# TensorE's opening filler: products of a cleared tile in place of transposes of the identity

## The chip, the cores and the metric

The kernel runs on one core of one Trainium2 chip. The metric is the device time of one execution in microseconds (us), as the median of several runs; the profile is a further execution, recorded by the hardware profiler, with a time of its own. Engines are named as in the profile: PE is TensorE's matmul, PEld its weight load, DVE is VectorE, ACT ScalarE, POOL GpSimd and SP the engine that issues most transfers.

## The reference

A stack of four graph layers over `x` of 128 batches, 128 nodes and 512 features, with one 128x128 matrix `adj`, all in float32. After each layer comes a layer norm of the sum:

```python
x = _layernorm(x + _L0_gnn_ref(x, adj, weight, bias))      # (adj @ x) @ W + bias
x = _layernorm(x + _L1_gnn_ref(x, W, a, beta, adj))        # graph attention, one head, masked by adj, elu
x = _layernorm(x + _L2_gnn_ref(x, adj, adj, b))            # max over nodes of relu(adj @ x + b)
x = _layernorm(x + _L3_gnn_ref(x, w_qkv, w_proj, ...))     # 8-head attention, masked by adj, projection, norm
```

For the opening of the kernel only the first layer counts: `y = einsum('nm,bmd->bnd', adj, x)`, then `einsum('bnd,do->bno', y, weight)`.

## The kernel before, in words

A batch is one tile of 128 partitions (nodes) by 512 features. Every batch is a chain of steps, written as a Python generator (`batch`) that yields a request for an engine with an estimated duration. A planner, `Plan.run`, serves the requests at build time in the order of its estimates, and so fixes the order of instructions on PE, DVE, ACT, POOL and SP. Each engine works through its own list in that order and waits on semaphores only for data and for free buffers. There are eight PSUM banks (`ps`).

The opening of the kernel runs like this. POOL builds a 128x128 identity, `ident`, with `make_identity` (a memset, then an affine select). SP issues the load of `adj` (`loads`, line 340), then those of the first weight `w0` in four chunks, while ACT's queue issues the load of batch 0 of `x` (line 332). `adjacency` (lines 388 to 402) takes a PSUM bank that nothing reads, calls `fill(10)`, and then transposes `adj_sb` on TensorE (line 395); `fill(2)` follows it in PE's list. DVE copies the transpose out of PSUM to `adjT` (line 398).

`mixed` (line 263) makes `adj @ x` of a batch, turned: four products of 128x128 by 128x128 (line 268), copied out of PSUM to `yT`. For batch 0 (`first`) there is again a `fill(2)` behind the products in PE's list, and DVE copies one half of `yT` (line 274) and ACT the other (line 276). `product` (line 260) then multiplies `yT` by `w0`, four products with 512 columns, each behind the landing of its chunk of `w0`.

`fill(n)` (line 383) issues n transposes of `ident` into the idle bank; nobody reads what they write:

```python
        for i in range(n):
            nc.tensor.transpose(idle[0][:, i % K, :], ident, ident)
```

The profile counts hardware instructions: a float32 product of the source is two of them (the four of line 268 for one batch are x8 in the timeline), each with a weight load of its own; a transpose is one (`fill(10)` is x10).

The requests of `adjacency` and `mixed` carry fixed durations (2.0 us for the opening on PE) that do not depend on what `fill` issues.

Of the kernel before, what the change touches and what calls it, by code (L numbers as in the profile page):

```python
# [8 lines left out]
F32 = mybir.dt.float32  # L9
# [6 lines left out]
P = 128  # L16
D = 512
K = D // P
# [30 lines left out]
class Plan:  # L49
# [14 lines left out]
    def use(self, engine, work, take=None, late=0.05, urgent=False, follow=False):  # L64

        names = take if callable(take) else lambda: (take,) if take else ()  # L70
        return engine, work, names, late, 0 if follow else 1 if urgent else 2
# [4 lines left out]
    def done(self, event, late=0.0):  # L76
        event.left -= 1
        event.at = max(event.at, self.now + late)
        if not event.left:
            for r in event.chains:  # L80
                r["ready"] = max(r["ready"], event.at)
                self.step(r, None)

    def give(self, slot):
        name, i = slot
        self.slots[name][i] = self.now
# [52 lines left out]
def gnn_stack_kernel(  # L139
# [17 lines left out]
    nc = tc.nc  # L157
# [3 lines left out]
    const = ctx.enter_context(tc.tile_pool(name="const", bufs=1))  # L161
# [8 lines left out]
    def buf(slot, *shape):  # L170
        return work.tile([P, *shape], F32, name="{}_{}".format(*slot))

    def bank(slot, *shape):

        p = ps.tile([P, D], F32, name="{}_{}".format(*slot))
        if len(shape) == 1:
            return p[:, : shape[0]]
        return p.rearrange("p (a b) -> p a b", a=shape[0])
# [84 lines left out]
    def mixed(xb, nodes, first=False):  # L263

        b0, b1 = yield use("PE", 0.9, lambda: ("ps", "yT"), late=0.2)
        p = bank(b0, K, P)
        for k in range(K):
            nc.tensor.matmul(p[:, k, :], xb[:, k * P : (k + 1) * P], nodes, start=True, stop=True)  # L268
        yT = buf(b1, K, P)
        if first:  # L270
            fill(2)

            yield use("DVE", 0.35, late=0.0)
            nc.vector.tensor_copy(yT[:, : K // 2], p[:, : K // 2])  # L274
            yield use("ACT", 0.05, urgent=True)
            nc.scalar.copy(yT[:, K // 2 :], p[:, K // 2 :])
        else:
            yield use("ACT", 0.6, urgent=True)
            nc.scalar.copy(yT, p)  # L279
        give(b0)  # L280
        return yT, b1
# [7 lines left out]
        nc.sync.dma_start(dst, scratch.rearrange("(a r) c f -> (r c) a f", a=Q))  # L289


    ident = const.tile([P, P], F32, name="ident")
    make_identity(nc, ident)
    neghalf = const.tile([P, 1], F32, name="neghalf")
# [86 lines left out]
    idle = []  # L381

    def fill(n):

        for i in range(n):
            nc.tensor.transpose(idle[0][:, i % K, :], ident, ident)  # L386

    def adjacency():
        b0 = yield use("PE", 2.0, "ps")
        idle.append(bank(b0, K, P))  # L390
        fill(10)
        yield adj_in
        b1 = yield use("PE", 0.3, "ps", late=0.2, urgent=True)
        p = bank(b1, K, P)
        nc.tensor.transpose(p[:, 0, :], adj_sb, ident)  # L395
        fill(2)
        yield use("DVE", 0.3)
        nc.vector.tensor_copy(adjT, p[:, 0, :])
        give(b1)
        done(adj_ready)  # L400
        give(b0)
        yield scalars_in
        yield use("DVE", 1.2)
        nc.vector.tensor_copy(adj_cols, adj_sb.rearrange("p (r c) -> p c r", c=Q))
        nc.vector.tensor_copy(ident_cols, ident.rearrange("p (r c) -> p c r", c=Q))
        nc.vector.tensor_scalar(
            maskb, adj_cols.rearrange("p c r -> p (c r)"), 0.0, MASKED,
            op0=ALU.is_equal, op1=ALU.mult,
        )
        nc.vector.tensor_scalar(  # L410
            beta_id, ident_cols.rearrange("p c r -> p (c r)"), beta1_sb, None, op0=ALU.mult
        )
# [273 lines left out]
    def batch(i):  # L686
# [5 lines left out]

        yield adj_ready
        yT, by = yield from mixed(xb, adjT, i == 0)
        biased = Event()
        plan.start(pool_add(xb, bias0_sb, biased, bias0_in), i)
# [19 lines left out]

        yield gr.attention[h]
        yT, by = yield from mixed(xb, gr.eT[h][:, b % 2])
        gr.read(h, 2)
        bp = yield use("PE", 3.44, "ps", late=0.2)  # L720
# [204 lines left out]
    with tc.manual_schedule(  # L925
        engines={ENG.PE, ENG.DVE, ENG.Activation, ENG.Pool, ENG.SP}
    ):
        plan.start(loads(), 0)
        plan.start(adjacency(), 0)
        for i in range(NB):  # L930

            plan.start(batch(i), early(i))
        plan.run()
# [27 lines left out]
```

## Time and profile before

| | |
|---|---|
| median of 4 runs | 3243.22 us (3243.09 to 3243.61) |
| profiled execution, time | 3243.25 us |
| profiled execution, span (first to last instruction) | 3241.5 us |
| PE busy | 3229.5 us of the span, 12831 instructions |
| PEld busy | 1724.3 us |
| DVE, ACT, POOL busy | 2660.8, 1176.2, 950.7 us |
| mean granted TensorE clock | 0.999 |

The span is 1.75 us shorter than the execution's time; the rest lies before the first and after the last instruction. The profiled execution stands within 0.03 us of the median. In a timeline row the first number is the start in us from the span's start, the second the time from the start of the row's first instruction to the end of its last (they overlap), then engine, line, operation, output<-inputs, shapes and the number of instructions; in brackets is the idle time before it and what ended it.

### The profile page before, as it was taken

Reading aid. Unit: us, or ns where it says so; the run is one execution under the profiler, and the core shown is the slowest. Engines: PE = TensorE matmul, PEld = TensorE weight load, DVE = VectorE, ACT = ScalarE, POOL = GpSimd, SP = SyncE. Lnnn points to the kernel's source line nnn. Section 1 sums busy time; section 2 is a strip of 40 time slices with the busy share of each in tenths; the row PEclk is TensorE's granted clock in tenths of the full one; section 3 lists DMA queues with packets and bytes.
Section 4 is the critical chain, followed back from the end, with each engine's and each line's share of the span. In section 5 each row is a group of like instructions: output and inputs, shape, how many; then the busy total and the mean of one; then the engine's idle time right before and its main releaser. Section 6 shows DMA issues by size and latency. Waiting matters only on the chain.

```text
span 3241.5 us, 40472 instructions
## 1 busy us (share of the span) xinstructions
PE 3229.5 (100%) x12831; PEld 1724.3 (53%) x12831; DVE 2660.8 (82%) x5677; ACT 1176.2 (36%) x3449; POOL 950.7 (29%) x1033
## 2 busy tenths in 40 slices
PE   9999999999999999999999999999999999999998
PEld 5655555545555455554555545555555555556565
DVE  7888788888888888888888888888787887888877
ACT  2433334333333333332333423334233342343332
POOL 3222223232232322323223232232232332233222
PEclk9999999999999999999999999999999999999999
DMA  4233322323323233232332323322333223332332
GB/s 173 55 97 106 106 75 77 101 91 106 92 70 98 94 106 92 70 95 95 106 104 65 88 95 107 101 71 82 99 104 107 71 77 101 99 111 66 116 88 96
DMA packets 469893, 304.27 MB, mean 94 GB/s; under 512 B 319280, under 2 KB 401584, under 8 KB 469680
## 3 DMA queue, kind: packets, MB, share of 16 engines
q1 hardware_dynamic: 469536, 301.42, 31.2%
q8 instruction: 103, 1.69, 0.2%
q14 instruction: 110, 0.90, 0.1%
q10 hardware_dynamic: 144, 0.26, 0.0%
HBM read 158.93 MB, written 142.67 MB: 93 GB/s over the span
## 4 chain that ended last, share of the span: by engine, by line
PE 100%; DVE 0%; POOL 0%; ACT 0%; issue 0%; POOLq 0%; DVEq 0%; ACTq 0%
PE ps L260 54%; PE ps L573 27%; PE ps L268 7%; PE ps L622 4%; PE ps L643 4%; PE ps L738 3%; PE ps L876 0%; PE ps L386 0%; ACT v L818 0%; POOL rstd L203 0%; PE ps L431 0%; DVE x L906 0%; DVE st L910 0%; POOLq L957 0%; PE ps L395 0%
## 5 line engine op out<-in xcount | busy, mean ns | idle before, releaser
L260 PE MATMUL ps<-w_sb,yT 128*128 128x512 f32 x2048 | 902.5, 592 | 0.2 <-DVE yT L274 0.2
L573 PE MATMUL ps<-xT,wqkv_sb 128*128 128x512 f32 (+1 forms) x2304 | 886.4, 545 | 0.0
L203 POOL TENSOR_TENSOR rstd<-ve,neghalf 128x1 f32<-128x1 f32 x640 | 436.0, 682 | 1152.2 <-DVE ve L197 942.3
L573 PEld LDWEIGHTS ps<-xT,wqkv_sb 128*128 128x128 f32 x2304 | 437.7, 190 | 446.8 <-issue 421.4
L260 PEld LDWEIGHTS ps<-w_sb,yT 128*128 128x128 f32 x2048 | 384.2, 190 | 458.6 <-issue 441.6
L260 PE MATMUL ps<-wqkv_sb,xT 128*128 128x512 f32 x1024 | 451.4, 593 | 0.0
L260 PE MATMUL ps<-wproj_sb,v 128*128 128x512 f32 x1016 | 445.5, 595 | 0.7 <-ACT v L818 0.7
L788 ACT ACTIVATE qkT<-qkT,nmx 128x128 f32<-128x128 f32 x1008 | 389.0, 389 | 16.4 <-DVE nmx L774 16.4
L189 DVE BATCH_NORM_STATS2 st<-x 128x6 f32<-128x512 f32 x510 | 347.3, 681 | 18.0 <-ACT x L746 15.1
L582 ACT ACTIVATE qkT<-ps 128x512 f32<-128x512 f32 (+1 forms) x144 | 77.4, 549 | 707.4 <-PE ps L573 707.4
L253 POOL TENSOR_TENSOR x<-x,v 128x512 f32<-128x512 f32 x127 | 174.1, 1371 | 516.4 <-DVE v L837 516.1
L260 PEld LDWEIGHTS ps<-wproj_sb,v 128*128 128x128 f32 x1016 | 190.7, 190 | 233.8 <-issue 229.9
L260 PEld LDWEIGHTS ps<-wqkv_sb,xT 128*128 128x128 f32 x1024 | 191.8, 190 | 227.8 <-issue 223.2
L253 POOL TENSOR_TENSOR x<-x,bias_sb 128x512 f32<-128x512 f32 x128 | 180.9, 1427 | 429.4 <-PE ps L268 419.1
L223 ACT ACTIVATE x<-x,nmr,rstd 128x512 f32<-128x512 f32 x257 | 206.6, 810 | 200.8 <-DVE nmr L221 194.8
L279 ACT COPY yT<-ps 128x512 f32<-128x512 f32 x255 | 147.6, 584 | 275.6 <-PE ps L268 275.6
L798 DVE STREAM_TRANSPOSE pt<-qkT 128x1024 f32<-128x1024 f32 x128 | 158.5, 1238 | 79.5 <-DMA p_d<-pt 79.2
L253 POOL TENSOR_TENSOR x<-x,beta_sb 128x512 f32<-128x512 f32 x128 | 163.0, 1274 | 186.6 <-DVE xt L753 142.6
L710 DVE SCALAR_TENSOR_TENSOR scr<-x,wa_rows 128x512 f32<-128x512 f32 x256 | 185.0, 722 | 26.3 <-ACT x L223 21.5
L788 ACT ACTIVATION_READ_ACCUMULATOR qkT<-qkT,nmx 128x1 f32 x1008 | 190.1, 189 | 0.0
L767 DVE TENSOR_TENSOR qkT<-ps,maskb 128x512 f32<-128x512 f32 x256 | 160.1, 681 | 29.2 <-PE ps L622 29.2
L726 ACT ACTIVATE ex<-ps 128x512 f32<-128x512 f32 x128 | 76.2, 595 | 241.1 <-PE ps L260 238.8
(86 smaller groups left out, 3513.9 us busy)
## 6 DMA issues: line engine op xcount, KB each, us to landing
p_d<-pt SPq DMA_DIRECT2D x128, 512.0 KB, 2.8
qkT<-p_d SPq DMA_DIRECT2D x128, 512.0 KB, 4.3
x_d<-xt SPq DMA_DIRECT2D x128, 256.0 KB, 2.3
xT<-x_d SPq DMA_DIRECT2D x512, 64.0 KB, 2.4
x<-in_x SPq DMA_DIRECT2D x127, 256.0 KB, 2.6
out<-x SPq DMA_DIRECT2D x127, 256.0 KB, 2.0
z<-s_d SPq DMA_DIRECT2D x64, 128.0 KB, 2.9
e_d<-et SPq DMA_DIRECT2D x64, 128.0 KB
```

The source lines that it names most:

```text
L189: nc.vector.bn_stats(st, src)
L203: nc.gpsimd.tensor_tensor(rstd, ve, neghalf, op=ALU.pow)
L223: nc.scalar.activation(xb, xb, AF.Identity, bias=nmr, scale=rstd)
L253: nc.gpsimd.tensor_tensor(dst, dst, other, op=ALU.add)
L260: nc.tensor.matmul(p, lhs(k), rhs(k), start=(k == 0), stop=(k == K - 1))
L268: nc.tensor.matmul(p[:, k, :], xb[:, k * P : (k + 1) * P], nodes, start=True, stop=True)
L279: nc.scalar.copy(yT, p)
L573: nc.tensor.matmul(p[:, j, :], wqkv_sb[:, k, (c + j) * P : (c + j + 1) * P], gr.xT[:, k, : gr.size * P], start=(k == 0), stop=(k == K - 1),)
L710: nc.vector.scalar_tensor_tensor(scr, xb, 1.0, wa_rows[:, j, :], op0=ALU.mult, op1=ALU.mult, accum_out=gr.s[:, b, j : j + 1],)
L767: nc.vector.tensor_tensor(pr[:, j * K : (j + 1) * K], sc[j], maskb[:, None, :].to_broadcast([P, K, P]), op=ALU.add,)
L788: nc.scalar.activation(pr[:, j, :], pr[:, j, :], AF.Exp, bias=nmx[:, j : j + 1], accum_out=sums[:, j : j + 1],)
L798: nc.vector.transpose(pt.rearrange("p c h s -> p h c s"), pr.rearrange("p h (c r) -> p h c r", c=Q))
```

## The change

A tile `zeros` of 128x128 is allocated and cleared by DVE ahead of everything else. `fill` issues products of `zeros` with its own first 64 columns in place of transposes of `ident`. The three calls of it grow from 10, 2 and 2 to 12, 3 and 3. The order of all other instructions, on every engine, is as before; DVE's list has the memset in front.

```diff
+    zeros = const.tile([P, P], F32, name="zeros")
+    nc.vector.memset(zeros, 0.0)
     ident = const.tile([P, P], F32, name="ident")
     make_identity(nc, ident)
...
     def fill(n):
 
         for i in range(n):
-            nc.tensor.transpose(idle[0][:, i % K, :], ident, ident)
+            nc.tensor.matmul(
+                idle[0][:, i % K, : P // 2], zeros, zeros[:, : P // 2], start=True, stop=True
+            )
 
     def adjacency():
         b0 = yield use("PE", 2.0, "ps")
         idle.append(bank(b0, K, P))
-        fill(10)
+        fill(12)
         yield adj_in
         b1 = yield use("PE", 0.3, "ps", late=0.2, urgent=True)
         p = bank(b1, K, P)
         nc.tensor.transpose(p[:, 0, :], adj_sb, ident)
-        fill(2)
+        fill(3)
...
         yT = buf(b1, K, P)
         if first:
-            fill(2)
+            fill(3)
```

## The prediction

> **What bounds the kernel now.** I read the page first: busy time, then the chain that ended last.
>
> ```profile
> span 3241.5 us, 40472 instructions
> PE 3229.5 (100%) x12831; PEld 1724.3 (53%) x12831; DVE 2660.8 (82%) x5677; ACT 1176.2 (36%) x3449; POOL 950.7 (29%) x1033
> PE 100%; DVE 0%; POOL 0%; ACT 0%; issue 0%; POOLq 0%; DVEq 0%; ACTq 0%
> ```
>
> PE is the chain. The table of waits for PE alone says where it ever stood still:
>
> ```profile
> PE ps L386 <- POOL ident masks.py:199: 1.4, 1, 1.4
> PE ps L260 <- ACT v L818: 0.7, 1, 0.7
> PE ps L876 <- ACT v L818: 0.7, 1, 0.7
> PE ps L260 <- DVE yT L274: 0.2, 1, 0.2
> ```
>
> These are 3.0 us in all: two at the start and two in the last twenty microseconds. Between 7.25 and 3222 us PE never waits, so whatever the change does to the moment at which the first product of L260 starts (7.25 us) is handed to the end one for one, and it can do nothing else: the filler stands only ahead of that moment. The question is when that product starts. The timeline of PE and of its weight loads over the opening, with two rows from further down:
>
> ```profile
> 1.39 2.39 PE L386 MATMUL ps<-ident 128*128 128x128 f32 x10 [1.39 <-POOL ident masks.py:199]
> 3.80 0.18 PEld L395 LDWEIGHTS ps<-ident,adj_sb 128*128 128x128 f32 x1 [0.43 <-DMA adj_sb<-in_adj]
> 3.80 0.47 PE L395 MATMUL ps<-ident,adj_sb 128*128 128x128 f32 x1
> 4.07 0.63 PE L386 MATMUL ps<-ident 128*128 128x128 f32 x2
> 4.32 0.29 DVE L398 COPY adjT<-ps 128x128 f32<-128x128 f32 x1 [4.32 <-PE ps L395]
> 4.66 2.08 PE L268 MATMUL ps<-adjT,x 128*128 128x128 f32 x8
> 6.53 0.53 PE L386 MATMUL ps<-ident 128*128 128x128 f32 x2
> 6.78 0.42 DVE L274 COPY yT<-ps 128x256 f32<-128x256 f32 x1 [2.17 <-PE ps L268]
> 7.25 0.30 PEld L260 LDWEIGHTS ps<-w_sb,yT 128*128 128x128 f32 x2 [0.49 <-DVE yT L274]
> 10.79 2.84 PE L268 MATMUL ps<-adjT,x 128*128 128x128 f32 x24
> 3228.91 3.72 PE L876 MATMUL ps<-wproj_sb,v 128*128 128x256 f32 x16 [0.74 <-ACT v L818]
> ```
>
> The reader is to see a slow clock in the opening. The same products of L268 take 2.84 us for 24 at 10.79 us (one takes 0.275, so 23 steps of 0.111) and 2.08 us for 8 at 4.66 us: steps of 0.213 between all but the first two. The transposes step by 0.213 too. The trace's record of the granted clock begins at 6.81 us, with full clock; ahead of that it has no record, so the page's clock row shows full there as well, and the steps are the better witness. I call 0.213 cold and 0.111 warm.
>
> **The filler's start.** It waits for DVE's memset, not for `ident`. After the same opening barrier POOL starts its memset of the same shape at 0.73 us, for 0.20; DVE has nothing ahead of its own. 0.73 + 0.20, and 0.05 from POOL's end to the first transpose as seen, gives 0.98 us, 0.4 earlier than 1.39 (bounds 0.85 to 1.08, by DVE rows of this shape of 0.1 less or more). DVE's first other work is at 4.32, so the memset costs nothing there.
>
> **What one filler costs.** This decides. A product of the source is two instructions, so `fill(12)` is 24 where there were 10, and each `fill(3)` is 6 where there were 2. Each has a weight load and a moving pass, and the load of the next runs beside the pass of this one, so the step is the longer of the two. The pass follows the width: 16 products of 256 columns took 3.72 us (0.216 each, warm), 128 columns 0.111, so 64 columns would be 0.054 warm and 0.107 cold. The load does not shrink: the stationary side is still all 128 columns. The two loads at 7.25 us, which nothing delays, span 0.30 us at 0.19 for one: the second begins 0.11 after the first, so a warm product load holds the path 0.11, and cold twice that, 0.21. So I take 0.111 warm and 0.213 cold for each, as if the width had not been halved. The other bound is the pass, 0.054 and 0.107. I am near the load since every product has one and its row is of the very same size.
>
> [...]
>
> **The opening, added up.** Cold, 24 fillers end at 0.98 + 24 x 0.213 = 6.09 us. In the trace before, `adj` is there at 3.80 us and its transpose starts then; the new filler stands in front of it in PE's list. If the clock rises at time R, then (R - 0.98)/0.213 fillers ran cold and the rest take 0.111 each. From the filler's end F on, all warm: transpose 0.11, six fillers 0.67, so L268 starts at F + 0.78 (the copy to `adjT` would allow 0.65: transpose 0.27, DVE 0.29, 0.09 for two hand-overs; the fillers are late). Then 8 x 0.111 = 0.89, and the half copy of `yT` ends 0.16 + 0.04 + 0.42 later and hands over in 0.05: 1.56; the six fillers behind them end at 0.89 + 0.67 = 1.56, the same. So L260 starts at F + 2.34, against 7.25 before.
>
> When is R? The trace bounds it. Before, the clock rose 5.43 us after the first transpose but only 2.15 us after the first product (4.66). If products alone count, R is 0.98 + 2.15 = 3.13 us; if the moment belongs to the chip's own pacing, or all PE work counts alike, it is 6.4 to 6.8. I take the middle of 3.13 and 6.81, 4.97 us, being near to neither: 18.7 fillers cold, 5.3 warm, F = 5.55, L260 at 7.89: 0.64 us later than before. At R = 3.13: 10.1 cold, 13.9 warm, F = 4.67, L260 at 7.01, 0.24 earlier. At R = 6.81: F = 6.09, the next six fillers begin at 6.36, two run cold and four warm, L268 starts at 7.24 and L260 at 8.80, 1.55 later.
>
> [...]
>
> What else moves: the loads of `w0` and `x` have the same issue order; a later PE finds them landed. The identity leaves the filler's start and becomes a second wait of L395, which it precedes by more than 2 us. The order on every engine is otherwise unchanged. So the sum is 3243.25 + 0.64 = 3243.9 us, and by the median of 3243.22 the same.
>
> A difference under 0.2% (6.5 us) can't be told from no change here; all cases below are inside it.
>
> **The rivals.** *One, the clock does not come earlier* (products of zeros, with the array moving half the time, count no more than transposes did, or the moment isn't the program's to choose): the change then doesn't do what it says, and the 24 fillers at 0.213 hold `adj`'s transpose from 3.80 to 6.09. Price +1.55 us, 3244.8. For it: the loads fill half of each step. Against: PE is busy without a gap from 0.98 on. It decides when R is later than 6.1. *Two, the filler is as cheap as its width* (0.107 cold): 24 end at 3.55, before `adj` is there, and the clock is up by then or soon after. L395 starts at 3.80 as before, L268 0.65 later, L260 at 6.01 at best, 1.24 earlier; batch 2 of `x`, which landed at 10.62 and whose products would be wanted at 10.44, takes 0.2 of that back. Price -1.1, 3242.1. For it: 0.43 us of PE's weight queue stood idle before 3.80, room that such a filler fits. Against: the load's row above. *Three, slower than can be missed*: the new tile shifts the addresses of all tiles behind it; if that cost 2 ns on each of PE's 12831 steps, 26 us, the kernel would be slower by 0.8%. It decides from 0.5 ns a step on (6.5 us). Nothing in the trace points to it; steps of one shape at different buffers agree to 1 or 2 ns.
>
> **How the numbers follow.** My forecast (load price, R between 3.1 and 6.1, -0.25 to +1.2): 0.57. Rival one: 0.25. Rival two: 0.16. Rival three: 0.02. The range leaves out the lower half of rival two and the far end of rival one and adds 0.25 for the scatter of the runs: 3242.4 to 3245.1. Faster by over 0.2%: 0.01; within: 0.97; slower: 0.02.
>
> **What would show it.** In the profile after: the first filler near 0.98 us; two weight loads per filler at steps of 0.21 and then 0.11, no step near 0.05; L395 starting clearly behind 3.80, at 4.7 to 6.1; L268's 8 products in about 1.05 us, not 2.08; L260 at 7.0 to 8.8; the record of the clock beginning ahead of 6.81. L395 still at 3.80 with idle time before it would make the price wrong; L268 still at 2.08 us would make the clock wrong; any difference beyond 7.25 to 3222 us would make the frame wrong.

## The result and the profile after

The changed kernel takes 3246.86 us (median of 41 runs, 3246.03 to 3247.56) against 3243.13 us of the kernel before in 61 runs alternating with it (3242.21 to 3245.01): ratio 1.0011, interval 1.0007 to 1.0016. It is 3.7 us slower, nearly six times the forecast difference, under the 0.2% that the prediction called a change but clear of the scatter (the two sets of runs do not overlap), and above the stated range of 3242.4 to 3245.1. The profiled execution took 3246.89 us with a span of 3245.1 us, 3.64 us more than the one before.

PE's waits show that the frame of the prediction holds. The only one left in the opening is the memset; the two near the end stand as before:

```profile
PE ps L388 <- DVE zeros L293: 1.1, 1, 1.1
PE ps L880 <- ACT v L822: 0.7, 1, 0.7
PE ps L260 <- ACT v L822: 0.7, 1, 0.7
```

The timeline of the opening after (lines moved: the filler is L388, `adj`'s transpose L399, the copy to `adjT` L402):

```profile
0.83 0.17 DVE L293 MEMSET zeros<- 128x128 f32 x1 [0.83 <-PEq L952]
1.05 5.38 PE L388 MATMUL ps<-zeros 128*128 128x64 f32 x24 [1.05 <-DVE zeros L293]
6.23 0.42 PE L399 MATMUL ps<-ident,adj_sb 128*128 128x128 f32 x1
6.44 1.38 PE L388 MATMUL ps<-zeros 128*128 128x64 f32 x6
7.61 2.02 PE L268 MATMUL ps<-adjT,x 128*128 128x128 f32 x8
9.43 1.38 PE L388 MATMUL ps<-zeros 128*128 128x64 f32 x6
10.60 3.97 PE L260 MATMUL ps<-w_sb,yT 128*128 128x512 f32 x8
14.40 2.84 PE L268 MATMUL ps<-adjT,x 128*128 128x128 f32 x24
```

All 24 fillers ran at the cold step of 0.213 us, so did the six behind L399, the products of L268 (2.02 us, as slow as before) and the next six. The trace's record of the granted clock begins at 11.23 us, with full clock; before it began at 6.81. This start is called the rise of the clock below. PE had work without a gap from 1.05 us on, and the clock came 4.4 us later than before.

Everything is lost ahead of the row at 14.40, which stood at 10.79 before: 3.61 us. In pieces: L399 starts 2.43 later (6.23 against 3.80); from there to L268 it takes 1.38 and not 0.86, 0.52 more; from L268 to L260 2.99 and not 2.59, 0.40 more; and the eight products of L260 take 0.26 more, since the first still ran cold. These are the 3.61.

### The profile page after: what moved, and what is told of

Its sections match the earlier page's. It is cut to its first block, busy times and chain, and to the rows that moved or that the text cites. A ratio compares the mean times of both kernels' runs of the same rounds, so it can differ in the third digit from the quotient of the medians.

```text
span 3245.1 us, 40518 instructions
## 1 busy us (share of the span) xinstructions
PE 3233.7 (100%) x12853; PEld 1729.4 (53%) x12853; DVE 2663.2 (82%) x5678; ACT 1176.1 (36%) x3449; POOL 950.9 (29%) x1033
## 4 chain that ended last, share of the span: by engine, by line
PE 100%; DVE 0%; ACT 0%; POOL 0%; issue 0%; POOLq 0%; DVEq 0%; ACTq 0%
PE ps L260 54%; PE ps L577 27%; PE ps L268 7%; PE ps L626 4%; PE ps L647 4%; PE ps L742 3%; PE ps L388 0%; PE ps L880 0%; ACT v L822 0%; POOL rstd L203 0%; PE ps L435 0%; DVE x L910 0%; DVE st L914 0%; POOLq L961 0%; DVE st L896 0%
## 5 line engine op out<-in xcount | busy, mean ns | idle before, releaser
L260 PE MATMUL ps<-w_sb,yT 128*128 128x512 f32 x2048 | 902.8, 592 | 0.0
L260 PEld LDWEIGHTS ps<-w_sb,yT 128*128 128x128 f32 x2048 | 384.4, 190 | 458.2 <-issue 442.2
L260 PE MATMUL ps<-wqkv_sb,xT 128*128 128x512 f32 x1024 | 451.4, 593 | 0.0
L260 PE MATMUL ps<-wproj_sb,v 128*128 128x512 f32 x1016 | 445.5, 595 | 0.7 <-ACT v L822 0.7
L260 PEld LDWEIGHTS ps<-wproj_sb,v 128*128 128x128 f32 x1016 | 190.7, 190 | 233.8 <-issue 230.4
L260 PEld LDWEIGHTS ps<-wqkv_sb,xT 128*128 128x128 f32 x1024 | 191.8, 190 | 227.8 <-issue 223.4
```

The costliest lines, as they stand in the source:

```text
L260: nc.tensor.matmul(p, lhs(k), rhs(k), start=(k == 0), stop=(k == K - 1))
```

## The experiments

**Theories.** The prediction's step for the moment of the clock had failed; I had let it be 6.81 us at the latest. Three explanations were open: A, products of cleared data do not count for the clock; B, passes of half width leave the array idle half of the time and so do not count enough; C, the filler never matters. Each run's time and ratio stand against the kernel before on the same chip: 3242.77 us for the first four runs, 3243.00 for the next four, 3243.01 for the last four.

**Zeros at full width.** Five, one and one calls are as many instructions as the transposes were.

```diff
-            nc.tensor.matmul(idle[0][:, i % K, : P // 2], zeros, zeros[:, : P // 2], ...)
+            nc.tensor.matmul(idle[0][:, i % K, :], zeros, zeros, start=True, stop=True)
-        fill(12) ... fill(3) ... fill(3)
+        fill(5) ... fill(1) ... fill(1)
```

> The filler is products of zeros over all 128 columns, 5, 1 and 1 calls (10, 2 and 2 instructions, as many as the transposes before). Theory A (cleared data does not count for the clock, at any width): the clock rises only after about 2 us of work on real data, which starts near 4.7 us, so between 6.5 and 9.9 us; time 3243 to 3244.6, median near 3243.9. Theory B (zeros would count, but half-width passes leave the array idle half of the time): the clock is up by 3 to 6.3 us, time 3242.0 to 3243.0. Theory C (no filler matters, the moment is chance): as A.

Measured: 3242.91 us (3242.17 to 3243.29), before 3242.77 (3242.19 to 3243.46); ratio 1.0000, 0.9991 to 1.0009. The clock rose at 6.03 us. With cleared data the clock came no later than with the transposes (6.81 us).

**Other data at full width.** As above, with

```diff
-    nc.vector.memset(zeros, 0.0)
+    nc.vector.memset(zeros, 1.3717421)
+    nc.vector.memset(zeros.rearrange("p (a b) -> p a b", b=2)[:, :, 1], -2.7182818)
```

> As the run with zeros over 128 columns, but the tile holds 1.3717421 and -2.7182818 in alternating columns. A and B: the clock is up by 3 to 6.3 us, time 3242.0 to 3243.0, median near 3242.3. C: 3243 to 3244.6, as with zeros.

Measured: 3243.07 us (3242.55 to 3243.24), ratio 1.0000 (0.9991 to 1.0010), clock at 7.06 us. No gain over zeros; clock and median lie outside what A and B both expected (at most 6.3 us and 3243.0).

**Other data at half width.** The changed kernel with this memset.

> The changed kernel (12, 3 and 3 calls of 64 columns) with the alternating values in place of zeros; nothing else differs. A: the clock rises at 3 to 6.3 us, part of the 24 fillers runs at 0.111, L395 starts at 4.7 to 6.1, time 3242.9 to 3244.6. B and C: 3246.9, clock at 9.4 to 12.7 us, as the changed kernel.

Measured: 3247.26 us (3246.43 to 3247.75), ratio 1.0013 (1.0004 to 1.0023), clock at 12.14 us. At half width the data make no difference that these runs can tell either: L399 and L260 start 0.19 us later than in the changed kernel, which is the second memset's delay of the filler, and the rest is the later clock (L260 takes 4.33 us and not 3.97), within what the changed kernel's own runs scatter. A falls.

**No filler.** `fill(0)` at all three places.

> The filler is left out altogether. If the transposes of the identity did count: slower than before by 0.5 to 1 us, clock at 6.5 us or later. If they did not: the same as before, 3243.1.

Measured: 3245.95 us (3244.70 to 3246.24), ratio 1.0010 (1.0000 to 1.0019), clock at 11.59 us. The transposes before were worth about 3 us (3.18 by the medians), three times or more what was expected; the slowest run of the kernel before, 3243.46, lies under the fastest without filler. So C falls. The rows of this run:

```profile
3.67 0.45 PE L399 MATMUL ps<-ident,adj_sb 128*128 128x128 f32 x1 [3.67 <-DMA adj_sb<-in_adj]
4.50 2.08 PE L268 MATMUL ps<-adjT,x 128*128 128x128 f32 x8 [0.38 <-DVE adjT L402]
7.09 5.92 PE L260 MATMUL ps<-w_sb,yT 128*128 128x512 f32 x8 [0.52 <-DVE yT L274]
```

In the kernel before, the last of these rows is:

```profile
7.25 3.70 PE L260 MATMUL ps<-w_sb,yT 128*128 128x512 f32 x8 [0.20 <-DVE yT L274]
```

Without filler L260 starts 0.16 us sooner, and then spends 5.92 us on what takes 3.70 warm. With the half-width filler of the changed kernel the clock came at 11.23, about as late as with no filler at all, though the two are not quite alike: the changed kernel starts L268 3.1 us later.

**Width and length apart.** What was left of the three is B: a filler whose moving pass (PE's row of a product, as against PEld's row, the load of its weights) is half as wide brings the clock later. Its rival L said that width is nothing and only the length of the filler costs. First the half width alone (64 columns; 5, 1 and 1 calls):

> Zeros, 64 columns, but 5, 1 and 1 calls (10, 2 and 2 instructions), so L395 is not held back. [...] Theory L (only the length of the filler costs, its width is nothing to the clock): as before, median 3242.8.

Measured: 3244.20 us (3243.63 to 3244.61), before 3243.00 (3242.27 to 3243.41); the clock rose at 9.99 us. Beside the run with no filler, where L268 starts at nearly the same time (4.50 against 4.62), this is about 2 us better: 1.20 over the kernel before and not 3.18. So a filler of half width falls short of the full one, but it is not worth nothing. Then the length alone (128 columns; 12, 3 and 3 calls):

> Zeros, all 128 columns, 12, 3 and 3 calls (24, 6 and 6 instructions), as many as in the changed kernel. [...] L: as the changed kernel, median 3246.9.

Measured: 3244.71 us (3243.81 to 3245.18), clock at 5.77 us. Neither range meets that of before, though the intervals of the ratios (0.9995 to 1.0013 and 0.9996 to 1.0014) reach 1. Its timeline is the one that the prediction had in mind for the change:

```profile
1.05 5.18 PE L388 MATMUL ps<-zeros 128*128 128x128 f32 x24 [1.05 <-DVE zeros L293]
6.07 0.27 PE L397 MATMUL ps<-ident,adj_sb 128*128 128x128 f32 x1
6.18 0.83 PE L388 MATMUL ps<-zeros 128*128 128x128 f32 x6
6.85 1.06 PE L268 MATMUL ps<-adjT,x 128*128 128x128 f32 x8
7.74 0.83 PE L388 MATMUL ps<-zeros 128*128 128x128 f32 x6
8.42 2.84 PE L260 MATMUL ps<-w_sb,yT 128*128 128x512 f32 x6
```

The fillers end almost as late as in the changed kernel, but behind them everything is warm: L268 in 1.06 us, and 2.35 us from L397 to L260 where the changed kernel needs 4.37. So the width alone costs 1.20 us, the length alone 1.71, and both together 3.73: 0.8 more than their sum. The traces show where: in the changed kernel the six cold fillers behind L399 end 0.59 us after the copy of `adjT` would have let L268 start, and the six behind L268 0.46 after the copy of `yT` would have let L260 start (with 0.05 for the hand-over in both). With the length alone, where these are warm, it is 0.13 and 0.01; with the width alone, where they are two, 0.01 and 0.01.

**Half the weights too.** Here the weights are narrowed to 64 columns as well:

```diff
+                idle[0][: P // 2, i % K, : P // 2], zeros[:, : P // 2], zeros[:, : P // 2], ...
```

> Zeros, 64 columns moving and 64 columns of weights too, 12, 3 and 3 calls. Load and pass are then equally long, so the step should halve to 0.107 cold, 24 fillers end near 3.7 us, ahead of adj, and the passes follow each other without a gap. [...] Theory S (what counts is how much of the array is filled, and half the columns are too few): clock at 9 us or later, time 3244 or more.

Measured: 3243.06 us (3242.45 to 3243.49), ratio 1.0000 (0.9990 to 1.0010); clock at 5.31 us.

```profile
1.05 2.82 PE L388 MATMUL ps<-zeros 128*64 128x64 f32 x24 [1.05 <-DVE zeros L293]
3.81 0.48 PE L399 MATMUL ps<-ident,adj_sb 128*128 128x128 f32 x1
4.21 0.90 PE L388 MATMUL ps<-zeros 128*64 128x64 f32 x6
5.04 1.27 PE L268 MATMUL ps<-adjT,x 128*128 128x128 f32 x8
```

24 fillers in 2.82 us are steps of 0.107, half of what the same pass cost behind a full load. They end ahead of `adj`, and with the clock at 5.31 us, ahead of the 6.03 behind the zeros at full width, theory S, which put it at 9 us or later, falls. There is no gain over the kernel before, since L268 starts at 5.04 and not at 4.58, as behind the zeros at full width: the step from L399 to the first narrow filler is 0.40 us, that from the last one to L268 0.24.

**Three quarters of the width.** 96 columns moving, 128 of weights; 5, 1 and 1 calls.

> Zeros, 96 columns moving, 128 of weights, 5, 1 and 1 calls: the pass runs three quarters of each step. [...] L: 3242.8.

Measured: 3244.01 us (3243.21 to 3244.71), ratio 1.0003 (0.9994 to 1.0013), clock at 8.72 us: between the full (6.03) and the half width (9.99), and every run above the 3242.8 of L, which falls. Each of these moments is from one trace; by the medians three quarters of the width cost 1.01 us over the kernel before, half cost 1.20, and the full width 0.14.

**The narrow filler where it costs nothing.** Narrow weights in the opening call alone; the two later ones over 128 columns, once each.

> The opening filler as 12 calls of zeros with 64 columns of weights and 64 moving (step 0.107), the two later fillers as one call each over 128 columns, so that no change of the weights' width stands ahead of L268. [...] Theory S: no gain over before.

Measured: 3242.73 us (3242.36 to 3243.32), before 3243.01 (3242.22 to 3243.36), ratio 0.9999 (0.9991 to 1.0008). The median lies 0.28 us under that of the kernel before; whether it is faster can't be told.

```profile
4.67 1.16 PE L268 MATMUL ps<-adjT,x 128*128 128x128 f32 x8
6.34 3.70 PE L260 MATMUL ps<-w_sb,yT 128*128 128x512 f32 x8 [0.29 <-DVE yT L274]
```

In this execution the clock rose at 4.19 us and L260 started 0.91 us ahead of before; the execution took 3242.50 us, 0.75 less than 3243.25.

**Long transposes.** The old filler, but 24, 6 and 6 transposes of the identity; the cleared tile stays, unused.

> Transposes of the identity as before, but 24, 6 and 6 of them. If transposes count for the clock as products do: as with products of zeros over 128 columns in the same number (3244.7), a little later for the start at 1.39: 3245.0. If they count for nothing: the clock waits for L268 as in the changed kernel, 3246.9 or more.

Measured: 3244.91 us (3243.70 to 3245.22), ratio 1.0006 (0.9996 to 1.0015), clock at 6.53 us, and L268 warm:

```profile
7.32 1.06 PE L268 MATMUL ps<-adjT,x 128*128 128x128 f32 x8
```

L397 starts at 6.55 us, so nothing but transposes of the identity had run when the clock rose. In these runs transposes brought it up as products over 128 columns did: 3244.71 and 3244.91 differ by no more than the 0.34 us of later start.

**The same kernels once more**, for the moment of the clock.

> The changed kernel once more, for the moment of the clock. [...] If the moment were fixed by the program: 11.23 again.

> The kernel before once more. [...] If fixed: 6.81.

Measured, one execution each: the changed kernel 3246.78 us with the clock at 11.03 us, the kernel before 3243.14 us with the clock at 7.21 us. The moment moved by 0.2 and 0.4 us. In the changed kernel the time followed by half of it (0.11 for 0.20); in the kernel before `adj` also landed 0.12 earlier, so no such reading is possible. Two repeats do not show how far it moves from run to run, or why. By the steps each cold microsecond loses 0.102 of 0.213, or 0.48 us; if the moment alone made the 1.53 us between the fastest and the slowest of the 41 runs, it would wander over an estimated 3.2 us, which no trace shows. The kernel before has more scatter: nine of its 61 runs lie at 3244.13 to 3245.01, apart from the other 52 (3243.73 at most); none of the nine was traced.

**The passes and the moment of the clock.** The traces side by side, by the rise of the clock. The step is that of the opening's filler, cold. The pass is an estimate: 0.107 us for 64 columns, which is the step behind weights as narrow, and in proportion 0.160 for 96 and 0.213 for 128.

| filler | step, us | pass, us | clock rises at, us |
|---|---|---|---|
| narrow weights, in the opening call alone | 0.107 | 0.107 | 4.19 |
| narrow weights, long | 0.107 | 0.107 | 5.31 |
| zeros, full width, long | 0.213 | 0.213 | 5.77 |
| zeros, full width, short | 0.213 | 0.213 | 6.03 |
| transposes, long | 0.213 | 0.213 | 6.53 |
| transposes (kernel before) | 0.213 | 0.213 | 6.81; again 7.21 |
| dense values, full width, short | 0.213 | 0.213 | 7.06 |
| three quarters, short | 0.213 | 0.160 | 8.72 |
| half width, short | 0.213 | 0.107 | 9.99 |
| half width, long (changed kernel) | 0.213 | 0.107 | 11.23; again 11.03 |
| dense values, half width, long | 0.213 | 0.107 | 12.14 |
| none | | | 11.59 |

In the eight traces in which the filler's pass fills its step the clock rose at 7.21 us at the latest, in the five in which it leaves part of the step free at 8.72 at the earliest. In the changed kernel PE's records leave no gap from 1.05 us to the rise at 11.23, so a PE that is never idle was not enough to bring the clock up by 7.21 us.

## Why the prediction was wrong

*What bounds the kernel* was right: PE never waits between its first L260 and the last 20 us, and the 3.61 us at 14.40 came out as 3.64 at the end.

*The filler's start* was right within its bounds, 1.05 us for 0.98. *The cost of one filler*, the step on which I spent most care, was right: 0.213 us cold, set by the load, not by the halved pass (with the load narrowed too it was 0.107). 24 of them held L399 back to 6.23, where the cold sum said 6.09. Rival two, a filler as cheap as its width, falls for the same reason; the run with narrow weights shows what it would have needed.

*The moment of the clock, R,* is the step that failed. I bounded it by 3.13 and 6.81 us and took the middle, 4.97; it was 11.23. The upper bound was the moment of before, reached on the ground that at worst the new filler would count as the old one did. But the fillers differ in just what went with the moment in the runs. The transposes step by 0.213 with a pass of an estimated 0.213, so the passes are back to back; the new product has the same step with a pass of 0.107, so the passes run half of the time. I had both numbers in the same paragraph and used them for the step alone. Rival one named this difference ("the array moving half the time", "the loads fill half of each step") and gave it 0.25, but priced it at the old moment of 6.81, +1.55 us. In the changed kernel the clock was still down when the fillers handed the opening to L268, which starts 3 us later than before (7.61 against 4.66) and is itself followed by six more such fillers.

That the rest of the sum held is shown by the run with the full width and the same length: its clock rose at 5.77 us, inside my bounds, and the prediction's sum at that R gives 22.5 cold and 1.5 warm fillers, F = 5.94, L260 at 8.28 and 3244.3 us; measured were 8.42 and 3244.49 in that execution.

With the half width, each of the terms behind R came out cold: the six fillers behind L399, counted at 0.67, took 1.17 (6.44 to 7.61) and held L268 back; the 1.03 us that a warm L268 was to return stayed lost; and the six behind it, counted as hidden, let L260 start 0.46 us after the 10.14 that the copy of `yT` allowed (it ended at 9.67 + 0.42, and 0.05 for the hand-over):

```profile
9.67 0.42 DVE L274 COPY yT<-ps 128x256 f32<-128x256 f32 x1 [2.70 <-PE ps L268]
```

*Rival three* (addresses of tiles) has nothing for it: the zeros at full width hold the same tile and time as before.

The lower bound of R, 3.13 us, rested on products alone bringing up the clock. The long transposes contradict that: clock at 6.53 us, ahead of any product, and L268 in 1.06 us. *Against* rival one I had set that PE is busy without a gap; it was, and the clock came at 11.23. That the moment goes by the share of a step that the pass fills is my inference from the shapes tried here, and no trace shows it directly.

## What to carry to other kernels

Here the clock rose by 7.21 us behind fillers with the moving side as wide as the weights (64 over 64, 128 over 128), and at 9.99 or later with 64 over 128, in the changed kernel at 11.23 with PE never idle from 1.05 on. So compare a filler's pass with the weight load ahead of it, and try the moving side at the width of the weights first. A filler that stands in an in-order queue ahead of needed work has to end, at the cold step, before that work's data lands (24 at 0.213 us held L399 to 6.23, where `adj`'s transpose had started at 3.80); size it by instructions of the trace, not by calls of the source, since a float32 product is two (`fill(12)` is x24). And in a sum over an unknown moment, bound it from what would happen if the new work counted for nothing, not from what the old work achieved.

## What the runs showed of the hardware

- Between zeros and dense values the runs can't tell: 3242.91 and 3243.07 us at full width (clock at 6.03 and 7.06), 3246.86 and 3247.26 at half (11.23 and 12.14, there with 0.19 us of later start).
- The clock rose at 4.19 to 7.21 us in the eight traces in which the filler's pass fills its step, at 8.72 to 12.14 in the five in which it fills half or an estimated three quarters.
- Narrowing the moving side alone to 64 columns left a float32 step at 0.213 us cold (the changed kernel); narrowing both sides gave 0.107 (24 in 2.82 us).
- Between narrow and full weights one step was longer: 0.40 us from L399 to the first narrow filler, where 0.27 went from L395 to the first transpose behind it in the kernel before. One trace shows this, and not why.
- Without any filler the clock rose at 11.59 us, 4.5 us after L260 had begun at 7.09; the opening's filler is worth 3 us of 3243 (3.18 by the medians).
